# A spectral layer whose inverse-transform factors are made on 16 lines instead of being copied from 8 lines to 8 others

## Chip, cores and metric

The kernel runs on one core of a Trainium2 chip. The metric is the device time of one launch in microseconds (us): the median of several runs. The launch does the whole computation, and nothing is computed outside it.

## What is computed

The input x is 8 images of 8 channels of 512 x 512 in fp32. Two layers are applied, each to a group-normalised copy (4 groups of 2 channels) and added to its input. Layer 0 is the one that this change touches:

```
xs  = gn(x)[:, :, ::2, ::2]                        # 256 x 256
FW1 = rfft2(xs)                                    # only 8 row modes (0..3, -4..-1) x 4 column modes are used
out2[b,o,y,x] = sum_i FW1[b,i,y,x] * w[i,o,y,x]    # complex: a mix of the 8 channels, per mode
tmp = einsum('boxw,xz->bozw', out2, exp(lam1 * X)) # back to 512 rows
x2  = einsum('bozw,wi->bozi', tmp, exp(lam2 * T))  # back to 512 columns
x   = x + real(x2) / (256 * 256)
```

Layer 1 is a coupled map lattice (15 steps, each a 3x3 convolution per channel), a hidden 3x3 convolution to 128 channels with a 1x1 convolution back to 8, and a gate that mixes both; its result is added to the layer's input. Nearly all of the work is in layer 1.

## The kernel before, in words

**Stages of one image.** Each of the 8 images is an `Element`. Its layer 0 is a generator, `layer0`, that yields after each small piece of work. Its layer 1 is the lattice in two halves of four channels (`Half`; per half 15 steps over five sets k = 0..4 of 4 x 32 rows), 128 hidden rounds (`Hidden.round`, and `Hidden.point` after every two) and 43 gates (`Gate`).

**Ticks.** The time of an image is cut into 75 ticks. Tick t convolves the sets n = 2t and n = 2t + 1: n below 75 belongs to the first half, from 75 on to the second, with step n % 75 // 5 + 1 and set n % 5. The function `work` writes one tick: two convolutions (L533, TensorE), their settling (L588 on VectorE, L594 on ScalarE), transfers (`feed`, then `fetch`), up to two hidden rounds (L633, then L639 on ScalarE and L641 on VectorE), `squares`, then `others.first`, `Hidden.point` (L652) and `others.second`. The last two give left-over PSUM banks to the gates of the image before or to pieces of layer 0 of the image after. Pieces of layer 0 of the image after start at tick 24 (in the first image at once, as there are no gates to do). The order of each engine's instructions is the order of the source: `keep_order` ties every instruction to the one before it on its engine. There are four pairs of PSUM banks, named `pair`.

**The change of halves.** Ticks 35 to 37 run step 15 of the first half, and the second of tick 37's sets is already step 1 of the second half. In these ticks `leave` stores the finished sets (L574, `cml<-m`, four transfers for each set, issued one tick after the set), and `fetch` loads the drives of the second half (L491, `dE<-xn` and `dO<-xn`, eight transfers for each set). For each set of the second half, `square` takes a buffer for m from the pool `sets` (15 buffers, first in first out), clears the edge columns on GpSimd (L512) and squares the even drive into it on ScalarE (L513). Such a buffer is often one that a store L574 is still reading, so L512 waits for that store.

**One queue for transfers.** All transfers after the constants are issued by SyncE (SP), in the order of the source.

**The modes in layer 0.** For each channel L336 multiplies the image rows, as the stationary operand, with `dft_y`: 16 columns, 8 cosine and 8 negated sine columns, one per row mode. L340 copies the result to `mys`. After the statistics, L350 takes the mean out of row mode 0 and L353 scales. L361 makes the column modes: its stationary operand is 8 columns of `mys`, so the result lies on 8 lines (partitions), one per row mode. L366 copies it to `f`; `total` (L371, L375, L377) mixes channels on 8 lines, first the real part (`re`), then the imaginary (`im`). The inverse transform over rows (`over_rows`, L398) has a contraction of 16: lines 0 to 7 of `e1` are cosines, lines 8 to 15 sines. So its stationary operand `om` needs re and im on lines 0 to 7 (L387, L388) and -im and re on lines 8 to 15. L389 and L390 make the latter on lines 0 to 7 in `of_sin`, and a transfer on SP carries them to lines 8 to 15:

```
nc.sync.dma_start(out=om[8:, :, :8], in_=of_sin)   # L391
yield LATER
```

Then `over_rows(c)` runs L398 for channel c (the first channel in the tick's left-over slot right after; `LATER` only asks for the first bank of a slot), L402 on ScalarE copies the PSUM bank to `ty`, and `synthesis` (L430, L433, L435) adds the result to x. `om` holds 32 columns per channel, 8 of them used, the rest zero.

Of the kernel before, what the change touches and what calls it, by code (L numbers as in the profile page):

```python
# [35 lines left out]
F32 = mybir.dt.float32  # L36
AF = mybir.ActivationFunctionType
ALU = mybir.AluOpType
# [3 lines left out]
P = 128  # L42
C = 8
N = 512
NS = N // 2
# [40 lines left out]
def shape_constants():  # L86

    ky = np.array([0, 1, 2, 3, -4, -3, -2, -1])
    kx = np.arange(4)
    c = {}  # L90
    p, j = np.arange(P)[:, None, None], np.arange(2)[None, :, None]
    a = 2 * np.pi * ((ky * (2 * p + j)) % NS) / NS
    c["dft_y"] = np.concatenate([np.cos(a), -np.sin(a)], axis=2)
    a = 2 * np.pi * ((kx * (P * j + p)) % NS) / NS
    re = np.concatenate([np.cos(a), -np.sin(a)], axis=2)
    im = np.concatenate([np.sin(a), np.cos(a)], axis=2)
    c["dft_x"] = np.stack([re, im], axis=2)
    waves = np.zeros((8, 4))
    waves[:, 0] = ky / NS
    waves[:, 1] = np.concatenate([kx, -kx]) / NS  # L100
    waves[:4, 2] = 0.25
    c["waves"] = waves
    i, o = np.arange(P)[:, None] % SLAB, np.arange(SLAB)[None, :]
    c["shift"] = np.stack([i - o == d - 1 for d in range(3)], axis=1)
    p = np.arange(P)
    c["ends"] = np.stack([p % SLAB == 0, p % SLAB == SLAB - 1, p == 0, p == P - 1], axis=1)
    c["group_of"] = (np.arange(P)[:, None] % C) // 2 == np.arange(G)[None, :]
    return {k: np.ascontiguousarray(v, dtype=np.float32) for k, v in c.items()}
# [12 lines left out]
def view(t, offset, dims):  # L121

    return bass.AP(tensor=t.tensor, offset=t.offset + offset, ap=[list(d) for d in dims])
# [3 lines left out]
def conv_layers(ctx: ExitStack, tc: tile.TileContext, a, out):  # L127
    nc = tc.nc
# [3 lines left out]
    cp = ctx.enter_context(tc.tile_pool(name="const", bufs=1))  # L132
    dram = ctx.enter_context(tc.tile_pool(name="dram", bufs=1, space=bass.MemoryType.DRAM))
    sm = ctx.enter_context(tc.tile_pool(name="small", bufs=1))
# [22 lines left out]
    def row(shape, name):  # L157
        return wk.tile(shape, F32, tag="row", name=name, bufs=2)
# [19 lines left out]
    def load(name, shape):  # L178
        t = cp.tile(shape, F32, name=name)
        nc.scalar.dma_start(out=t, in_=a[name])  # L180
        return t
# [7 lines left out]
    xs_first = [load_x(sets, 0, c) for c in range(C)]  # L189


    dft_y = load("dft_y", [P, 2, 16])
    dft_x = load("dft_x", [P, 2, 2, 8])
    waves = load("waves", [8, 4])
    group_of = load("group_of", [P, G])
    ends = load("ends", [P, 4])
    w_p = load("w_p", [P, 3, 2, HID])
# [18 lines left out]

    e1 = cp.tile([16, N], F32, name="e1")
    e2 = cp.tile([P, N], F32, name="e2")
    om = cp.tile([16, C, 32], F32, name="om")
    nc.gpsimd.memset(om, 0.0)  # L220
    grid = {}
    for name in "XT":
# [3 lines left out]
    def sines():  # L226
        u, k, t = (sets.take([8, N], name) for name in ("u", "k", "sines"))
        rd = sm.tile([8, 1], F32, name="rd")
        for to, name, col, shift in (
            (e1[:8], "X", 0, 0.25), (t, "X", 0, 0.0), (e2[:8], "T", 1, waves[:, 2:3])  # L230
        ):
            xr = grid[name]
            nc.vector.tensor_tensor(rd, xr[:, 2:3], xr[:, 0:1], ALU.subtract)
            nc.vector.reciprocal(rd, rd)
            nc.vector.tensor_tensor(rd, rd, waves[:, col : col + 1], ALU.mult)
            nc.vector.tensor_scalar(u, xr, rd, shift, ALU.mult, ALU.add)
            nc.vector.tensor_scalar(k, u, MAGIC, None, ALU.add)
            nc.vector.tensor_scalar(k, k, MAGIC, None, ALU.subtract)
            nc.vector.tensor_tensor(u, u, k, ALU.subtract)
            nc.scalar.activation(to, u, AF.Sin, scale=6.283185)  # L240
        nc.scalar.dma_start(out=e1[8:], in_=t)
        for j in range(1, 4):
            nc.scalar.dma_start(out=e2[32 * j : 32 * j + 8], in_=e2[:8])
        for tile_ in (u, k, t, *grid.values()):
            sets.drop(tile_)
# [72 lines left out]
    def layer0(e, bank):  # L318


        def one():
            return bank[-1][:, 0]

        st = sm.tile([P, C, 4, 6], F32, name="st")
        mys = sm.tile([P, C, 2, 16], F32, name="mys")


        for c in range(C):
            yield c
            xt = e.x[c]  # L330
            for j in range(4):
                nc.vector.bn_stats(st[:, c, j], xt[:, j])
            my = one()[:, :32].rearrange("p (h k) -> p h k", h=2)
            for h in range(2):
                for j in range(2):
                    nc.tensor.matmul(  # L336
                        my[:, h], xt[:, 2 * j, h * NS : (h + 1) * NS : 2], dft_y[:, j],
                        start=(j == 0), stop=(j == 1),
                    )
            nc.scalar.copy(mys[:, c], my)  # L340
            e.done_with(c)
# [4 lines left out]
        lift = sm.tile([P, G], F32, name="lift")  # L346
        nc.vector.tensor_scalar(lift, mean, float(NS), None, ALU.mult)
        for g in range(G):
            at = mys[:, 2 * g : 2 * g + 2]
            nc.vector.tensor_scalar(  # L350
                at[:, :, :, 0], at[:, :, :, 0], lift[:, g : g + 1], None, ALU.subtract
            )
            nc.vector.tensor_scalar(at, at, rstd[:, g : g + 1], None, ALU.mult)  # L353
        wmix, ts = row([8, 2, C, C, 4], "wmix"), row([8, 2, C, C, 4], "ts")
        nc.sync.dma_start(out=wmix, in_=a["wmix"])
        yield LATER
        mx = one()[:, : C * 8].rearrange("p (c k) -> p c k", k=8)
        for c in range(C):
            for h in range(2):
                for q in range(2):  # L360
                    nc.tensor.matmul(  # L361
                        mx[:8, c], mys[:, c, h, q * 8 : (q + 1) * 8], dft_x[:, h, q],
                        start=(h + q == 0), stop=(h + q == 2),
                    )
        f = sm.tile([8, C, 2, 4], F32, name="f")
        nc.vector.tensor_copy(f, mx[:8].rearrange("p c (q k) -> p c q k", q=2))  # L366


        def total(q0, v0, q1, v1, op, name):
            for i, (q, v) in enumerate(((q0, v0), (q1, v1))):  # L370
                nc.vector.tensor_tensor(  # L371
                    ts[:, i], f[:, :, q].unsqueeze(2).to_broadcast([8, C, C, 4]), wmix[:, v],
                    ALU.mult,
                )
            nc.vector.tensor_tensor(ts[:, 0], ts[:, 0], ts[:, 1], op)  # L375
            t = sm.tile([8, C, 4], F32, name=name)
            nc.vector.tensor_reduce(t, ts[:, 0].rearrange("k i o m -> k o m i"), AX.X, ALU.add)  # L377
            return t

        yield LATER  # L380
        re = total(0, 0, 1, 1, ALU.subtract, "re")
        yield LATER
        im = total(0, 1, 1, 0, ALU.add, "im")

        of_sin = sm.tile([8, C, 8], F32, name="of_sin")
        s = 1.0 / (NS * NS)
        nc.vector.tensor_scalar(om[:8, :, 0:4], re, s, None, ALU.mult)  # L387
        nc.vector.tensor_scalar(om[:8, :, 4:8], im, s, None, ALU.mult)  # L388
        nc.vector.tensor_scalar(of_sin[:, :, 0:4], im, -s, None, ALU.mult)  # L389
        nc.vector.tensor_scalar(of_sin[:, :, 4:8], re, s, None, ALU.mult)  # L390
        nc.sync.dma_start(out=om[8:, :, :8], in_=of_sin)  # L391
        yield LATER


        def over_rows(c):
            ps = one()
            for at in range(0, P, 32):
                nc.tensor.matmul(  # L398
                    ps[at : at + 32], om[:, c], e1, start=True, stop=True, tile_position=(0, at)
                )  # L400
            ty = row([P, P, 4], "ty")
            nc.scalar.copy(ty.rearrange("k p j -> k (p j)"), ps)  # L402
            return ty
# [21 lines left out]
        def synthesis(ty, xt, st, half):  # L425
# [8 lines left out]
            for i in range(2):  # L434
                nc.vector.bn_stats(st[:, 2 * half + i], xt[:, 2 * half + i])  # L435

        ty_next = over_rows(0)
        closing = None
        for c in range(C):
# [416 lines left out]
    for i in range(3):  # L856
        xn = dram.tile([NP + 1, C, N], F32, name=f"xn{i}")
        cml, nca = (dram.tile([NP, C, N], F32, name=f"{name}{i}") for name in ("cml", "nca"))
        for plane in (xn, cml, nca):
            nc.scalar.dma_start(  # L860
                out=view(plane, 0, [[(NP - 1) * C * N, 2], [N, C], [1, N]]), in_=zrow
# [10 lines left out]
    for n in count():  # L872
        if n == C:
            sines()
            bands()
        if not e.pieces:
            break
        e.spectral(next(turns), 0, 0)
        tick()

        while e.stored >= C // 2 and len(e.first.loads) > 8 * (SETS - 2) and sets.free:
            e.first.load(nc.sync)
# [132 lines left out]
```

## Time and profile before

| what | value |
|---|---|
| median of 3 runs | 9992.99 us (9989.27 to 10003.49) |
| the profiled execution, its own time | 9988.58 us |
| its span | 9986.8 us |
| TensorE (PE) busy | 9359.6 us, 94% |
| VectorE (DVE) busy | 5869.1 us, 59% |
| ScalarE (ACT) busy | 4297.8 us, 43% |
| GpSimd (POOL) busy | 1755.5 us, 18% |
| mean granted TensorE clock | 0.983 |
| transfers by SyncE, share of the 16 DMA engines | 52.0% |

A line of the waits view says which engine and line waited, for whom, for how long in total, how often, and the longest of them. A line of the timeline gives start, duration, engine, line, operation, output<-inputs and count; in brackets stands the idle time of the engine just before it, and who ended it. `SPq` is SyncE issuing transfers; a DMA issue's duration is the issue alone.

### The profile page before, as it was taken

Reading aid. Unit: us, or ns where it says so; the run is one execution under the profiler, and the core shown is the slowest. Engines: PE = TensorE matmul, PEld = TensorE weight load, DVE = VectorE, ACT = ScalarE, POOL = GpSimd, SP = SyncE. Lnnn points to the kernel's source line nnn. Section 1 sums busy time; section 2 is a strip of 40 time slices with the busy share of each in tenths; the row PEclk is TensorE's granted clock in tenths of the full one; section 3 lists DMA queues with packets and bytes.
Section 4 is the critical chain, followed back from the end, with each engine's and each line's share of the span. In section 5 each row is a group of like instructions: output and inputs, shape, how many; then the busy total and the mean of one; then the engine's idle time right before and its main releaser. Section 6 shows DMA issues by size and latency. Waiting matters only on the chain. (4 is left out here: it accounts for less than half of the span.)

```text
span 9986.8 us, 353049 instructions
## 1 busy us (share of the span) xinstructions
PE 9359.6 (94%) x160496; PEld 4296.7 (43%) x160496; DVE 5869.1 (59%) x6067; ACT 4297.8 (43%) x4445; POOL 1755.5 (18%) x1406
## 2 busy tenths in 40 slices
PE   6999999899998999989999899999999899998999
PEld 2444444443444444444444444444434444444433
DVE  5665555665566655666556655566555565555555
ACT  2444444444444434444344443444434354344422
POOL 2010111103121031101312013120121202211212
PEclk9999999999999999999999999999999999999999
DMA  4241355447544565445665356552566526753688
GB/s 147 88 120 34 82 140 134 134 127 168 139 128 136 126 163 137 133 124 135 159 144 141 112 141 162 141 158 94 143 160 145 155 91 144 168 129 94 150 199 200
DMA packets 625562, 1353.48 MB, mean 136 GB/s; under 512 B 73066, under 2 KB 73194, under 8 KB 594050
## 3 DMA queue, kind: packets, MB, share of 16 engines
q1 hardware_dynamic: 621728, 1329.77, 52.0%
q8 instruction: 1261, 20.66, 0.9%
q14 instruction: 235, 1.93, 0.1%
q10 hardware_dynamic: 2338, 1.13, 0.0%
HBM read 992.27 MB, written 268.78 MB: 126 GB/s over the span
## 5 line engine op out<-in xcount | busy, mean ns | idle before, releaser
L533 PE MATMUL pair<-m,band 32*32 32x512 f32 x115200 | 4096.7, 605 | 200.2 <-issue 96.0
L594 ACT ACTIVATE m<-m 128x1024 f32<-128x1024 f32 x2240 | 2363.7, 1055 | 2795.7 <-DVE m L588 2674.2
L533 PEld LDWEIGHTS pair<-m,band 32*32 32x32 f32 x115200 | 2262.4, 103 | 1941.3 <-issue 970.0
L633 PE MATMUL pair<-cols,w_p 32*128 32x511 f32 (+1 forms) x24576 | 2866.2, 603 | 41.4 <-DMA cols<-xn 14.2
L588 DVE SCALAR_TENSOR_TENSOR m<-pair,dO 128x1024 f32<-128x1024 f32 x1280 | 1507.2, 1219 | 1478.0 <-PE pair L533 1294.2
L633 PEld LDWEIGHTS pair<-cols,w_p 32*128 32x128 f32 x24576 | 1270.8, 186 | 1651.0 <-issue 1123.3
L588 DVE SCALAR_TENSOR_TENSOR m<-pair,dE 128x1024 f32<-128x1024 f32 x1120 | 1319.1, 1219 | 1068.6 <-PE pair L533 878.3
L641 DVE TENSOR_SCALAR h<-pair,b_p 128x1024 f32<-128x1024 f32 x1024 | 1312.9, 1283 | 810.8 <-PE pair L633 803.3
L639 ACT ACTIVATE h<-pair,b_p 128x1024 f32<-128x1024 f32 x1024 | 1140.3, 1114 | 1043.4 <-PE pair L633 1043.0
L652 PE MATMUL pair<-h,w_u 128*32 128x512 f32 x8192 | 996.5, 598 | 136.4 <-DVE h L641 123.5
L726 POOL TENSOR_TENSOR mix<-mix 96x512 f32<-96x512 f32 x344 | 437.4, 1271 | 3757.9 <-ACT mix L724 3551.2
L703 PE MATMUL pair<-gin,w_g 128*32 128x511 f32 (+1 forms) x8256 | 964.1, 600 | 33.3 <-DMA gin<-nca 17.0
L708 POOL TENSOR_TENSOR mix<-mix 96x512 f32<-96x512 f32 x344 | 443.4, 1289 | 2050.6 <-DMA mix<-nca 1340.1
L598 POOL TENSOR_SCALAR dO<-dO 128x2048 f32<-128x2048 f32 x80 | 431.9, 5410 | 1225.6 <-DVE m L588 1225.5
L652 PEld LDWEIGHTS pair<-h,w_u 128*32 128x32 f32 x8192 | 249.4, 110 | 757.1 <-issue 384.0
L703 PEld LDWEIGHTS pair<-gin,w_g 128*32 128x32 f32 x8256 | 235.3, 110 | 711.2 <-issue 472.2
L665 ACT ACTIVATE y<-y,b_u 128x512 f32<-128x512 f32 x256 | 184.7, 721 | 808.0 <-DVE y L661 807.8
L731 DVE SCALAR_TENSOR_TENSOR mix<-mix,back 96x512 f32<-96x512 f32 x344 | 335.7, 976 | 148.5 <-POOL mix L726 148.5
L659 ACT COPY y<-pair 128x512 f32<-128x512 f32 x256 | 149.7, 585 | 605.1 <-PE pair L652 482.8
L713 DVE TENSOR_SCALAR mix<-pair,b_g 128x512 f32<-128x512 f32 x344 | 258.0, 750 | 251.6 <-PE pair L703 251.4
L720 PE MATMUL pair<-mix,w_g 128*32 128x512 f32 x2064 | 356.8, 593 | 9.6 <-DVE mix L713 7.8
L526 POOL TENSOR_SCALAR dO<-dO,base 128x512 f32<-128x512 f32 x320 | 237.0, 756 | 453.8 <-DMA dO<-xn 323.0
(86 smaller groups left out, 2643.8 us busy)
## 6 DMA issues: line engine op xcount, KB each, us to landing
gin<-xn SPq DMA_DIRECT2D x344, 384.0 KB
cols<-xn SPq DMA_DIRECT2D x256, 512.0 KB
x<-in_x SPq DMA_DIRECT2D x120, 1024.0 KB
gin<-cml SPq DMA_DIRECT2D x344, 320.0 KB
gin<-nca SPq DMA_DIRECT2D x344, 320.0 KB
dE<-xn SPq DMA_DIRECT2D x320, 256.0 KB
dO<-xn SPq DMA_DIRECT2D x320, 256.0 KB
mix<-xn SPq DMA_DIRECT2D x344, 192.0 KB
```

The lines of the kernel that those rows point to most:

```text
L533: nc.tensor.matmul(ps[h // 2][32 * t : 32 * t + 32, h % 2], band[at, c0 + (t if step % 2 else h), dx], m[at, t, dx : dx + N], start=(n == ...
L588: nc.vector.scalar_tensor_tensor(u[:, at], ps[q], FLOOR, d[:, at], ALU.max, ALU.add)
L594: nc.scalar.square(u[:, at], u[:, at])
L598: nc.gpsimd.tensor_scalar(d, d, 0.5, None, ALU.add)
L633: nc.tensor.matmul(ps[g // 2][:, g % 2, lo:hi], w_p[p, dx, i % 2], self.cols[p, i // 2, at : at + hi - lo], start=(n == 0), stop=(n == 2), ...
L639: nc.scalar.activation(h[:, :2], ps[0], AF.Relu, bias=b_p)
L641: nc.vector.tensor_scalar(h[:, 2:], ps[1], b_p, 0.0, ALU.add, ALU.max)
L652: nc.tensor.matmul(ps[32 * g : 32 * g + 32], w_u[:, r % 4], h[:, g], start=(r == self.hs[0][0]), stop=(r == self.hs[-1][0]), tile_position ...
L703: nc.tensor.matmul(ps[32 * j : 32 * j + 32, lo:hi], gband[:, dx], gin[:, j, at : at + hi - lo], start=(n == 0), stop=(n == 2), tile_positi ...
L708: nc.gpsimd.tensor_tensor(d, d, ng, ALU.subtract)
L720: nc.tensor.matmul(ps[at], gpoint[:, at], mix[:, 3], start=True, stop=True, tile_position=(0, 32 * j),)
L726: nc.gpsimd.tensor_tensor(d, d, mix[: GR * C, 2], ALU.mult)
```

## The change

The row modes are made twice: `dft_y` has each of its cosine and sine columns two times, so `mys` has 32 columns per half instead of 16, and L361's stationary operand has 16 columns, which puts the same modes on lines 0 to 7 and again on lines 8 to 15. `wmix`, `ts`, `f`, `re`, `im` get 16 lines. Two columns of constants, `on_cos` (1/NS^2 on lines 0 to 7, 0 elsewhere) and `on_sin` (-1/NS^2 on lines 8 to 15, 0 elsewhere), select what each line needs, so four VectorE instructions write all 16 lines of `om`. `of_sin` and the transfer of L391 are gone. `om` is packed to 8 columns per channel; L398 still reads 32 columns, of which 24 now belong to the next three channels (or to three channels of zeros at the end), and the lines of the result that they make are not read.

```diff
-    c["dft_y"] = np.concatenate([np.cos(a), -np.sin(a)], axis=2)
+    c["dft_y"] = np.concatenate([np.cos(a), np.cos(a), -np.sin(a), -np.sin(a)], axis=2)
...
+    waves[:8, 3] = 1.0 / (NS * NS)
+    waves[8:, 4] = -1.0 / (NS * NS)
...
-    om = cp.tile([16, C, 32], F32, name="om")
+    om = cp.tile([16, C + 3, 8], F32, name="om")
...
-        mys = sm.tile([P, C, 2, 16], F32, name="mys")
+        mys = sm.tile([P, C, 2, 32], F32, name="mys")
...
-            my = one()[:, :32].rearrange("p (h k) -> p h k", h=2)
+            my = one()[:, :64].rearrange("p (h k) -> p h k", h=2)
...
-                at[:, :, :, 0], at[:, :, :, 0], lift[:, g : g + 1], None, ALU.subtract
+                at[:, :, :, 0:9:8], at[:, :, :, 0:9:8], lift[:, g : g + 1], None, ALU.subtract
...
-        wmix, ts = row([8, 2, C, C, 4], "wmix"), row([8, 2, C, C, 4], "ts")
+        wmix, ts = row([16, 2, C, C, 4], "wmix"), row([16, 2, C, C, 4], "ts")
...
-                        mx[:8, c], mys[:, c, h, q * 8 : (q + 1) * 8], dft_x[:, h, q],
+                        mx[:16, c], mys[:, c, h, q * 16 : (q + 1) * 16], dft_x[:, h, q],
...
-        of_sin = sm.tile([8, C, 8], F32, name="of_sin")
-        s = 1.0 / (NS * NS)
-        nc.vector.tensor_scalar(om[:8, :, 0:4], re, s, None, ALU.mult)
-        nc.vector.tensor_scalar(om[:8, :, 4:8], im, s, None, ALU.mult)
-        nc.vector.tensor_scalar(of_sin[:, :, 0:4], im, -s, None, ALU.mult)
-        nc.vector.tensor_scalar(of_sin[:, :, 4:8], re, s, None, ALU.mult)
-        nc.sync.dma_start(out=om[8:, :, :8], in_=of_sin)
+        on_cos, on_sin = waves[:, 3:4], waves[:, 4:5]
+        back = sm.tile([16, C, 4], F32, name="back_re")
+        nc.vector.tensor_scalar(back, re, on_sin, -1.0, ALU.mult, ALU.mult)
+        nc.vector.tensor_scalar(re, re, on_cos, None, ALU.mult)
+        nc.vector.scalar_tensor_tensor(om[:, :C, 0:4], im, on_sin, re, ALU.mult, ALU.add)
+        nc.vector.scalar_tensor_tensor(om[:, :C, 4:8], im, on_cos, back, ALU.mult, ALU.add)
         yield LATER
...
-                    ps[at : at + 32], om[:, c], e1, start=True, stop=True, tile_position=(0, at)
+                    ps[at : at + 32], om[:, c : c + 4].rearrange("p c k -> p (c k)"), e1, start=True, stop=True, tile_position=(0, at)
```

The array `wmix` in memory holds its 8 lines twice. In the program's order the change leaves the number of instructions of TensorE, VectorE, ScalarE and GpSimd as it was and takes 8 issues, one per image, out of SP's queue.

More of the change, by code (lines that the diff above doesn't have):

```diff
@@ L97, in shape_constants @@
     c["dft_x"] = np.stack([re, im], axis=2)
-    waves = np.zeros((8, 4))
-    waves[:, 0] = ky / NS
-    waves[:, 1] = np.concatenate([kx, -kx]) / NS
+    waves = np.zeros((16, 5))
+    waves[:8, 0] = ky / NS
+    waves[:8, 1] = np.concatenate([kx, -kx]) / NS
     waves[:4, 2] = 0.25
+    waves[:8, 3] = 1.0 / (NS * NS)
+    waves[8:, 4] = -1.0 / (NS * NS)
     c["waves"] = waves
@@ L189, in conv_layers @@
     xs_first = [load_x(sets, 0, c) for c in range(C)]
-    dft_y = load("dft_y", [P, 2, 16])
+    dft_y = load("dft_y", [P, 2, 32])
     dft_x = load("dft_x", [P, 2, 2, 8])
-    waves = load("waves", [8, 4])
+    waves = load("waves", [16, 5])
     group_of = load("group_of", [P, G])
@@ L229, in sines @@
         for to, name, col, shift in (
-            (e1[:8], "X", 0, 0.25), (t, "X", 0, 0.0), (e2[:8], "T", 1, waves[:, 2:3])
+            (e1[:8], "X", 0, 0.25), (t, "X", 0, 0.0), (e2[:8], "T", 1, waves[:8, 2:3])
         ):
@@ L234, in sines @@
             nc.vector.reciprocal(rd, rd)
-            nc.vector.tensor_tensor(rd, rd, waves[:, col : col + 1], ALU.mult)
+            nc.vector.tensor_tensor(rd, rd, waves[:8, col : col + 1], ALU.mult)
             nc.vector.tensor_scalar(u, xr, rd, shift, ALU.mult, ALU.add)
@@ L361, in layer0 @@
                     nc.tensor.matmul(
-                        mx[:8, c], mys[:, c, h, q * 8 : (q + 1) * 8], dft_x[:, h, q],
+                        mx[:16, c], mys[:, c, h, q * 16 : (q + 1) * 16], dft_x[:, h, q],
                         start=(h + q == 0), stop=(h + q == 2),
                     )
-        f = sm.tile([8, C, 2, 4], F32, name="f")
-        nc.vector.tensor_copy(f, mx[:8].rearrange("p c (q k) -> p c q k", q=2))
+        f = sm.tile([16, C, 2, 4], F32, name="f")
+        nc.vector.tensor_copy(f, mx[:16].rearrange("p c (q k) -> p c q k", q=2))
         def total(q0, v0, q1, v1, op, name):
@@ L371, in total @@
                 nc.vector.tensor_tensor(
-                    ts[:, i], f[:, :, q].unsqueeze(2).to_broadcast([8, C, C, 4]), wmix[:, v],
+                    ts[:, i], f[:, :, q].unsqueeze(2).to_broadcast([16, C, C, 4]), wmix[:, v],
                     ALU.mult,
@@ L375, in total @@
             nc.vector.tensor_tensor(ts[:, 0], ts[:, 0], ts[:, 1], op)
-            t = sm.tile([8, C, 4], F32, name=name)
+            t = sm.tile([16, C, 4], F32, name=name)
             nc.vector.tensor_reduce(t, ts[:, 0].rearrange("k i o m -> k o m i"), AX.X, ALU.add)
@@ L992 @@
         "T": i["T"],
-        "wmix": w12.transpose(2, 4, 0, 1, 3),
+        "wmix": np.tile(w12.transpose(2, 4, 0, 1, 3), (2, 1, 1, 1, 1)),
         "K": i["K_local"].reshape(C, 9),
```

## Prediction

> **What bounds the kernel now.** First the page: TensorE (PE) is busy 94% of the span. Then the waits view for PE alone, as only what PE waits for can shorten the span, and its view by the tile `om`, which shows the operations around the removed transfer.
>
> ```profile
> PE 9359.6 (94%) x160496; PEld 4296.7 (43%) x160496; DVE 5869.1 (59%) x6067; ACT 4297.8 (43%) x4445; POOL 1755.5 (18%) x1406
> ```
>
> ```profile
> PE pair L652 <- DVE h L641: 123.5, 140, 1.6
> PE pair L398 <- DMA om<-of_sin: 117.1, 8, 24.4
> PE pair L533 <- issue: 96.0, 58, 5.2
> PE pair L533 <- ACT m L513: 64.8, 20, 10.6
> ```
>
> PE is idle 9986.8 - 9359.6 = 627 us in all, and 117.1 us of it is eight waits for the one transfer that the change removes. Asked window by window, they are 6.7 us (start, at 64 us), 3.0 (at 360 us), and then 15.1, 24.4, 18.8, 17.6, 15.1 and 16.4 us (images 1 to 6, sum 107.4). Why the last six are so long shows in the timeline of the first of them:
>
> ```profile
> 1840.92 0.16 DVE L387 TENSOR_SCALAR om<-re 8x32 f32<-8x32 f32 x1
> ...
> 1841.48 3.94 SPq L491 DMA_DIRECT2D dE<-xn  x4
> 1846.38 3.45 SPq L491 DMA_DIRECT2D dO<-xn  x4
> 1850.89 0.77 SPq L391 DMA_DIRECT2D om<-of_sin  x1
> 1851.95 7.63 SPq L574 DMA_DIRECT2D cml<-m  x8
> ...
> 1856.48 1.20 PE L398 MATMUL pair<-e,om 16*32 16x512 f32 x4 [15.13 <-DMA om<-of_sin]
> ```
>
> VectorE had the factors by 1841.8; the transfer of 2 KB stood in SP's queue behind eight drive loads, went out at 1850.9 and landed at 1856.4. The view by windows gives the DMA engines a share of 0.98 to 1.00 from 1800 to 1860 there: it is a burst of loads and stores at the change of halves. So the next question is what else PE needs from this burst. The same timeline, a tick later:
>
> ```profile
> 1860.38 0.11 POOL L512 MEMSET m<- 128x8 f32 x1 [17.09 <-DMA cml<-m]
> 1863.08 0.11 POOL L512 MEMSET m<- 128x8 f32 x1 [2.59 <-DMA cml<-m]
> ```
>
> ```profile
> 1872.10 3.88 ACT L513 ACTIVATE m<-dE,mhalf 128x2048 f32<-128x2048 f32 x2
> 1875.88 0.57 ACT L402 COPY ty<-pair 128x512 f32<-128x512 f32 x1
> ...
> 1876.51 4.10 PE L533 MATMUL pair<-m,band 32*32 32x512 f32 x116 [0.79 <-ACT ty L402]
> ```
>
> Tick 38's convolutions need two squares (L513), these need L512, and L512 waits for the stores L574. Today the second L512 is done at 1863.2 and its square is wanted at about 1874: the wait for `om` hides this one. The last image has no layer 0 after it, so no `om`, and shows what lies beneath:
>
> ```profile
> 9071.29 0.11 POOL L512 MEMSET m<- 128x8 f32 x1 [14.42 <-DMA cml<-m]
> 9071.43 2.00 ACT L513 ACTIVATE m<-dE,mhalf 128x2048 f32<-128x2048 f32 x1 [8.91 <-POOL m L512]
> ...
> 9073.49 9.25 PE L533 MATMUL pair<-m,band 32*32 32x512 f32 x192 [10.57 <-ACT m L513]
> ```
>
> [...] where the queue is free: from issue to PE's start took 2.2 us (61.98 to 64.22) and 2.0 us (357.91 to 359.91); in the burst it took 5.6. [...] after the wait of 15.1 us 183 records of L533 took 8.20 us, after the wait of 3.0 us 6.70 us. [...]
>
> **The change part by part.**
>
> *Removed:* eight L391 and their waits. *Taking their place at PE:* L398 waits for VectorE's four small instructions. L387 to L390 took 0.16 us each, about 0.1 us apart when nothing disturbs them; the two forms with a second tensor I price at L283's row (128x8, 0.222 us). So `om` is ready within 1 us of where `of_sin` was. PE's last work before the wait ended at 1841.3, the four would end at about 1841.8: 0.5 us at most instances, 1.5 in image 3, where L390 took 1.44 us. Queued behind L398 is all of PE, but in images 1 to 6 this half microsecond falls into the wait below.
>
> *Images 1 to 6, the new last wait.* PE resumes about 15 to 24 us earlier and does tick 37 without a new need of the burst: its sets were squared before, its columns (`cols`) loaded since 1820. In tick 38 its fifth record waits for L402 (`ty`), which stands on ScalarE behind both squares. From the second L512 on: 0.14 us to the square (9071.29 to 9071.43), 2.0 us for it, 0.57 us for the copy with 0.1 overlap, 0.05 to PE: 2.65 us. So tick 38 starts at (second L512) + 2.65 us at the earliest. Its start before, less that floor, is the gain if L512 doesn't move:
>
> | image | L533 after `ty` | second L512 | gain |
> |---|---|---|---|
> | 1 | 1876.51 | 1863.08 | 10.8 |
> | 2 | 3098.09 | 3082.49 | 13.0 |
> | 3 | 4323.89 | 4308.70 | 12.5 |
> | 4 | 5549.31 | 5535.07 | 11.6 |
> | 5 | 6767.36 | 6752.11 | 12.6 |
> | 6 | 7993.02 | 7977.85 | 12.5 |
>
> The sum is 73.0 us, each below its `om` wait, so the floor binds in all six. L574 stands right behind L391: with that gone it can be issued up to 1.06 us earlier (1850.89 against 1851.95)[...]. I take 0.7: + 4.2 us (1.2 to 6.4).
>
> *Slow restart.* PE now idles for some us at tick 38 and runs its first records at the low clock: 9.25 us for 192 records in the last image against 6.74 warm (at 7905), 2.5 us; the 15 us wait above cost 1.5[...]. I take 1.5 for each: - 9.0 us (0 to -16).
>
> *What is late next.* The squares of sets 3 and 4 (L513 at 1889.45) wait for the store of the first half's last set, which is issued after that tick's `cols` load. It comes earlier too, but meets the end of the burst: I put its landing at about 1872 to 1874 (it was 1879.5), and the squares shift to about 1877. Some 4 us remain, so 0; the other end is in the second rival.
>
> *Start and image 0.* At the start the chain is bare: 61.9 to 64.2, less four L353 that are longer by 64 elements [...]: + 2.0. In image 0: PE free at 356.9, `om` ready at about 358, before 359.9: + 1.8. Together 3.8.
>
> *Added PE work.* L336 has 512 records in all (16 columns more each). Eight took 1.11 us, 0.14 each; the load of 128 columns fills most of that. [...] 0 to 3.4 us, I take 1.7. L361: 64 pairs took 1.65 us (26 ns each), with 8 columns more to load[...]; 0 (up to 2). L340 gets 32 elements more, about 0.03 us on ScalarE (43% busy), nothing on the path; without that cover 64 x 0.03 = 2 us. [...] `om`'s packing leaves L398 at 32 columns: 0.
>
> *Sum:* 73.0 + 4.2 - 9.0 + 3.8 - 1.7 = 70 us (56 to 84 with the ends as I think they combine). The profiled execution's 9988.58 would become 9918; the median of the runs, 4.4 us above it, 9923.
>
> **The rivals.**
>
> *A, all of the wait goes.* If the stores land much earlier without L391, or buffers turn out to be others, PE gets 107.4 - 3 for `om`, + 3.8, + up to 9 for a clock that stays up: 108 to 117, so 9880. Against it speak the six L512 times and the last image. 6%.
>
> *B, more is given back.* The last image has a second wait of 5.45 us at 9088 for the squares of sets 3 and 4. If images 1 to 6 get it too, 6 x 5.45 = 33 us are lost: 9956, and up to 9971 with a second slow restart of 2.5 us each. Against it: here two hidden rounds (5.4 us) stand between the two convolutions, there they don't. 11%.
>
> *C, slower: the doubled row modes.* PE is the bound, and L336 grows. It eats the gain at 70/512 = 0.137 us more per record, and is slower by 0.2% from 0.176. An L336 record takes 0.268 us from end to end now and is issued every 0.14 us. Only if 16 columns more doubled that would this decide, say 10015. 3%.
>
> That the transfer isn't really removed is excluded by the program's order: SP has 8 issues less.
>
> **How the numbers follow.** My case has 80%, with 9909 to 9937 as its own range. The range of 8 in 10 takes in B's lower end and a little of the way to A: 9898 to 9957. 0.2% (20 us) is about what a measurement can tell here. My case, A and nearly all of B are faster by more: 0.93; 0.04 within; 0.03 slower.
>
> **What would show it.** Right: PE's waits no longer name `om<-of_sin`, L398 <- VectorE is below 10 us in all, and about 4 to 12 us of idle appear in each of images 1 to 6 before L533, released by ACT m L513 or ACT ty L402, with L512 still ended by `cml<-m`, the second of them within about 1 us of where it stood relative to the drive loads. L336's eight records stay at about 1.1 us. Wrong: no wait at L513 or `ty` (A), a second wait for L513 some 15 us later (B), L336 near 2 us (C), or L398 waiting several us for VectorE.

## The result and the profile after

The changed kernel took 9905.70 us (median of 4 runs, 9902.76 to 9917.57) beside 9998.24 us for the kernel before (4 runs, 9989.27 to 10005.24): ratio 0.9913, 95% interval 0.9902 to 0.9925. The profiled execution took 9903.73 us with a span of 9901.9 us, 84.9 us less than the span before. The prediction said 9923 us with a range of 9898 to 9957: the median lies inside it, and 3 us below the narrower range (9909 to 9937) that it gave its own case. In the changed kernel the lines after the constants stand two or three lower: L533 is L536, L512 is L515, L513 is L516, L398 is L401, L402 is L405, L652 is L655, L336 is L338, L361 is L363.

The page's first line, then the waits view for PE (us in total, number of waits, longest):

```profile
PE 9355.4 (94%) x160496; PEld 4299.0 (43%) x160496; DVE 5876.2 (59%) x6067; ACT 4301.9 (43%) x4445; POOL 1762.5 (18%) x1406
```

```profile
PE pair L655 <- DVE h L644: 124.7, 141, 1.9
PE pair L536 <- issue: 99.6, 59, 4.9
PE pair L536 <- ACT m L516: 69.7, 21, 11.8
PE pair L401 <- DVE om L393: 20.0, 8, 5.3
PE pair L536 <- ACT ty L405: 8.1, 6, 2.8
```

PE's work is what it was (9355 against 9360 us); its idle time fell from 627 to 546 us. The wait of 117.1 us for the transfer became one of 20.0 us for VectorE. Smaller increases stand beside it: the waits for L516 and `ty` together grew by 8.3 us (from 64.8 and 4.7), those put down to "issue" at L536 by 3.6 (by 13.0 over all lines of PE, from 110.7 to 123.7).

The timeline of image 1 shows the new wait for `om`:

```profile
1833.41 2.22 POOL L529 TENSOR_SCALAR dE<-dE,base_e 128x512 f32<-128x512 f32 x2 [2.27 <-ACT m L516]
1833.52 0.61 DVE L391 TENSOR_SCALAR re<-re,waves 16x32 f32<-16x32 f32 x1
...
1834.17 1.49 DVE L392 SCALAR_TENSOR_TENSOR om<-im,waves,re 16x32 f32<-16x32 f32 x1
1835.59 0.23 DVE L393 SCALAR_TENSOR_TENSOR om<-im,waves,back_re 16x32 f32<-16x32 f32 x1
1835.88 0.63 PE L401 MATMUL pair<-e,om 16*32 16x512 f32 x4 [2.20 <-DVE om L393]
```

and a tick later the floor that the prediction computed, the two clearings and what follows the second:

```profile
1853.07 0.11 POOL L515 MEMSET m<- 128x8 f32 x1 [17.44 <-DMA cml<-m]
...
1855.60 0.11 POOL L515 MEMSET m<- 128x8 f32 x1 [2.42 <-DMA cml<-m]
...
1855.74 2.00 ACT L516 ACTIVATE m<-dE,mhalf 128x2048 f32<-128x2048 f32 x1 [0.52 <-POOL m L515]
1857.65 0.56 ACT L405 COPY ty<-pair 128x512 f32<-128x512 f32 x1
...
1858.26 8.05 PE L536 MATMUL pair<-m,band 32*32 32x512 f32 x188 [1.08 <-ACT ty L405]
```

From the second clearing to PE: 1858.26 - 1855.60 = 2.66 us; predicted 2.65.

**A yardstick for all that follows.** In each of images 1 to 6, take the interval from the end of PE's last record before `om` (L655, until 1833.7 in image 1) to its first convolution record after `ty` (1858.3 there). The sum of the six is "inside", the rest of the span "outside". The start and image 0 count as outside.

| profiled execution | inside, us | PE idle inside | outside, us |
|---|---|---|---|
| before | 229.2 | 112.1 | 9757.6 |
| changed | 152.1 | 33.9 | 9749.8 |
| changed, two more executions | 146.9, 152.0 | 33.3, 39.6 | 9748.4, 9753.3 |

So 77.1 of the 84.9 us came from inside, 7.8 from outside. Of the 7.8, 5.2 us are time in which PE was busy (9242.4 and 9237.2 us outside), the rest idle time.

### The profile page after: what moved, and what is told of

The parts are those of the page before. It is cut to its first block, busy times and chain, and to the rows that moved or that the text cites. A ratio compares the mean times of both kernels' runs of the same rounds, so it can differ in the third digit from the quotient of the medians.

```text
span 9901.9 us, 353033 instructions
## 1 busy us (share of the span) xinstructions
PE 9355.4 (94%) x160496; PEld 4299.0 (43%) x160496; DVE 5876.2 (59%) x6067; ACT 4301.9 (43%) x4445; POOL 1762.5 (18%) x1406
## 3 DMA queue, kind: packets, MB, share of 16 engines
q8 instruction: 1261, 20.66, 0.9%
## 5 line engine op out<-in xcount | busy, mean ns | idle before, releaser
L536 PE MATMUL pair<-m,band 32*32 32x512 f32 x115200 | 4093.8, 605 | 212.5 <-issue 99.6
L536 PEld LDWEIGHTS pair<-m,band 32*32 32x32 f32 x115200 | 2258.3, 103 | 1955.8 <-issue 983.1
L636 PE MATMUL pair<-cols,w_p 32*128 32x511 f32 (+1 forms) x24576 | 2862.1, 603 | 47.0 <-issue 15.9
L655 PE MATMUL pair<-h,w_u 128*32 128x512 f32 x8192 | 995.0, 598 | 136.2 <-DVE h L644 124.7
L655 PEld LDWEIGHTS pair<-h,w_u 128*32 128x32 f32 x8192 | 249.0, 110 | 756.7 <-issue 384.7
L529 POOL TENSOR_SCALAR dO<-dO,base 128x512 f32<-128x512 f32 x320 | 238.6, 763 | 437.1 <-DMA dO<-xn 246.3
```

The source lines that it names most:

```text
L536: nc.tensor.matmul(ps[h // 2][32 * t : 32 * t + 32, h % 2], band[at, c0 + (t if step % 2 else h), dx], m[at, t, dx : dx + N], start=(n == ...
L636: nc.tensor.matmul(ps[g // 2][:, g % 2, lo:hi], w_p[p, dx, i % 2], self.cols[p, i // 2, at : at + hi - lo], start=(n == 0), stop=(n == 2), ...
L655: nc.tensor.matmul(ps[32 * g : 32 * g + 32], w_u[:, r % 4], h[:, g], start=(r == self.hs[0][0]), stop=(r == self.hs[-1][0]), tile_position ...
```

## The experiments

The theory was the prediction's: the transfer is late because it stands behind the drive loads on SP's queue and meets full DMA engines (a share of 0.98 to 1.00 there), and what the change gains is cut by the clearing of m. The rivals: the transfer itself is what costs; the doubled modes cost; something else takes the time back. All ratios are to the kernel before on the same chip. The runs of the kernel before had medians of 9989.91, 10004.15 and 9991.21 us in the three groups in which the experiments ran.

**1. The transfer kept, from another queue** (before, L391 issued by ScalarE):

```diff
-        nc.sync.dma_start(out=om[8:, :, :8], in_=of_sin)
+        nc.scalar.dma_start(out=om[8:, :, :8], in_=of_sin)
```

> The kernel before with one word changed: the transfer of the sines' factors is issued by ScalarE instead of SP. Theory (the transfer was late because of its place in SP's queue): it goes out at once and lands 2 to 6 us after of_sin, so PE waits 2 to 6 us for it in images 1 to 6 instead of 15 to 24, the squares and the ty copy behind them then set the same floor as in the changed kernel, and the time falls by 70 to 95 us. Rival (the 16 DMA engines are full, so any transfer is late there): the waits stay above 10 us each and the gain is below 45 us.

Measured: 9942.12 us (4 runs), ratio 0.9954 (0.9938 to 0.997), a gain of 48 us: between the two. PE still waited 52.0 us for the transfer, in 7 waits. Its timeline, image 1 (`ACTq` is ScalarE issuing):

```profile
1840.93 0.73 ACTq L391 DMA_DIRECT2D om<-of_sin  x1
...
1846.44 1.20 PE L398 MATMUL pair<-e,om 16*32 16x512 f32 x4 [6.01 <-DMA om<-of_sin]
...
1847.46 9.39 PE L533 MATMUL pair<-m,band 32*32 32x512 f32 x183
```

The transfer was issued as soon as VectorE had written `of_sin` (0.03 us later in every image). In images 1 to 6 it then took 5.5 to 7.9 us from its issue to PE, with the DMA engines' share at 0.60 to 0.91 meanwhile; at the start and in image 0 of the kernel before it had taken 2.2 and 2.0 us, with a share of 0.02. In the kernel before, the transfer stood 61.7 us in SP's queue, summed over the six images (7.8 to 15.9 us each), and that is what the other queue took away: the six waits fell from 107.4 to 45.6 us. What is left is the flight past the other transfers, longer than the theory had it. PE came back slowly: 183 records in 8.1 to 9.4 us, waits for instructions left out, where 6.95 us is their time at the full granted clock. But so it did in the kernel before (8.1 to 8.7) and in five of the six images of the changed kernel (8.1 to 9.2; 6.95 in image 1), so this is not what sets the three apart. Inside fell to 175.5 us, 53.7 less than before; outside hardly moved (9759.5).

**2. The doubled modes alone** (changed kernel, but `om` from `re` and `im` on lines 0 to 7, and lines 8 to 15 by a transfer on SP again):

```diff
...
+        of_sin = sm.tile([8, C, 8], F32, name="of_sin")
+        s = 1.0 / (NS * NS)
+        nc.vector.tensor_scalar(om[:8, :C, 0:4], re[:8], s, None, ALU.mult)
...
+        nc.sync.dma_start(out=om[8:, :C], in_=of_sin)
```

> The changed kernel with its doubled row modes and 16 lines, but with om made on 8 lines and carried to lines 8 to 15 by the transfer on SP, as before. It measures the cost of the doubled modes alone. Theory: 0 to 5 us slower than the kernel before, PE's waits for om again 15 to 24 us in images 1 to 6. Rival (the wider modes cost TensorE or the copies something that the removed wait hides): 15 us slower or more.

Measured: 9988.29 us (12 runs) against 9989.91 (17 runs), ratio 0.9995 (0.9987 to 1.0004). The wait was back:

```profile
PE pair L402 <- DMA om<-of_sin: 103.2, 7, 20.4
```

So what the change adds costs nothing that can be told (13 us gained to 4 lost), though each L338 record took 282 ns where L336's took 268, and L363's weight loads 93 where L361's took 87. Rival C falls. The gain of the change comes from PE's not having to wait for the transfer.

**3. The changed kernel with the burst spread** (a call of `fetch` issues at most 8 drive loads; it had been up to 16):

```diff
-            while n >= -11 and self.loads and (self.loads[0][2] or sets.free):
-                self.load(nc.sync)
+            for _ in range(8):
+                if n >= -11 and self.loads and (self.loads[0][2] or sets.free):
+                    self.load(nc.sync)
```

> The changed kernel, with fetch issuing at most eight drive loads in a tick, so that the stores of the finished sets stand behind 8 loads in SP's queue instead of 16. Theory (what is left is the floor of the second clearing of m, which waits for those stores): the second clearing comes 6 to 9 us earlier relative to PE, PE's waits for the squares or ty in images 1 to 6 (10 us in all in the changed kernel's trace) go to below 3 us, the last image's wait of 19.8 us falls below 12, and the time falls by 8 to 25 us against the changed kernel. Rival (the burst is bound by its bytes, or the loads now come too late in the next tick): same as the changed kernel within 5 us, or slower with waits for dE or dO.

Measured: 9875.96 us (4 runs), ratio 0.9881 (0.9862 to 0.99), beside the changed kernel as it is:

> The changed kernel again, for a second trace and a tighter comparison on the same chip as the others. Expected 0.9913 of the kernel before within 0.0015; the first record of L401 waits about 2.2 us for VectorE in each of images 1 to 6 again if that wait has a cause in the program and isn't chance.

which took 9897.08 us (5 runs), ratio 0.9911 (0.9894 to 0.9927). The timeline of image 1 of the spread version (its second clearing, then tick 38; L516 here is the clearing):

```profile
1844.29 0.54 POOL L516 MEMSET m<- 128x8 f32 x1 [2.41 <-PE pair L537]
...
1854.42 0.56 ACT L405 COPY ty<-pair 128x512 f32<-128x512 f32 x1
1855.03 6.54 PE L537 MATMUL pair<-m,band 32*32 32x512 f32 x188 [0.79 <-ACT ty L405]
```

The second clearing began 10.7 us before tick 38, not 2.66; counted from the interval's start it came 8.3 to 11.9 us earlier than in the changed kernel (6 to 9 were expected). PE idled 0.8 us there (4.7 us in the six images, where below 3 was expected), the last image's waits for squares fell from 19.8 to 8.8 us, and no image restarted slowly (6.54 us for 188 records in four of them, the other two broken by a wait put down to "issue"). Inside fell from 152.1 to 131.6 us: the floor had cost the changed kernel 20 us, and a late store, not layer 0, set it. The gain of 21 us on the changed kernel is within what was expected.

**4. The same limit in the kernel before**, transfer and all:

> The kernel before with one edit: a call of the fetch issues at most 8 drive loads, so L391's transfer stands behind 8 loads on SP's queue and not 16, and its engines carry half the burst. Theory (the wait was the transfer's place in the queue plus full DMA engines, and the late clearing of m was the burst too): TensorE's wait for om falls from 117 us to 40-70 us and the time to 9925-9955 us, faster than the kernel with the transfer on ScalarE's queue or like it, but 50-80 us slower than the changed kernel with the same limit. Rival (the transfer itself[...] was the wait, or the burst doesn't matter to it): om wait stays above 90 us and the time within 20 us of the kernel before.

Measured: 9899.42 us (4 runs), ratio 0.9892 (0.9873 to 0.9911), as fast as the changed kernel without the limit (0.9911 to 0.9923). The waits for `om` behaved as the theory had it, the time did not: 25 us below its range.

```profile
PE pair L398 <- DMA om<-of_sin: 55.9, 8, 11.2
PE pair L534 <- ACT m L514: 55.3, 18, 5.5
```

Nor did the transfer stand behind 8 loads, as had been expected: in three of the six images it was issued 0.03 us after VectorE's work, and its time in the queue was 8.1 us in all, not 61.7. The changed kernel with the same limit was only 38 us faster (9861.60 us, see 5), not 50 to 80.

Run again beside the changed kernel, and with L391 on ScalarE as well:

> The kernel before with the limit of 8 loads, again, beside the changed kernel on the same chip, as its 105 us were far above what was expected. Theory (half the burst takes 61 us of the om wait, about 15 us of L534's wait for m, and the cold clock with them): ratio 0.988-0.990 again, level with the changed kernel or up to 15 us below it. Rival (its first run was favoured by chance): 0.992-0.994, where the expectation of its first run had it.

> The kernel before with both small edits: at most 8 drive loads in a call of the fetch, and L391 issued by ScalarE. Theory (of the transfer only its place in SP's queue and the full DMA engines cost time; with both eased the change has little left to bring): TensorE's wait for om falls to 25-40 us (2 to 6 us in each image) and the ratio to the kernel before to 0.985-0.988, level within 10 us with the changed kernel with the limit (0.986 and 0.9881). Rival (the transfer costs a full flight of 5.5 us and a cold clock in each image whatever its queue): om wait 45-55 us, ratio 0.989-0.991, level with the limit alone.

> The changed kernel as it is, on the same chip as the two others: ratio 0.990-0.992 as in its two first runs; om wait 20.0 us in 8 waits. If fetch stalls of TensorE are a property of the program and of its DMA load, L536's waits put down to issue are 96-106 us again, and all of 1 us or more of them lie on the same place of a 256-instruction grid.

Measured in one group: 9898.77 us, ratio 0.9909 (0.9892 to 0.9925), for the limit alone; 9897.74, ratio 0.9906 (0.9888 to 0.9924), with the other queue too; 9910.38, ratio 0.9923 (0.9907 to 0.9938), for the changed kernel. The second run of the limit alone fell just outside what the theory gave it (as did the changed kernel, 0.9923 against 0.990 to 0.992; its wait for `om` was 20.0 us again, and L536's "issue" waits 103.4); the gain of the limit is 92 to 105 us. The two edits together brought no more than one: the wait for `om` stayed where it was,

```profile
PE pair L398 <- DMA om<-of_sin: 54.5, 7, 10.7
```

so on the wait and the ratio the rival was right: with half the burst the queue place no longer matters (8.1 and 5.6 us in the two runs of the limit alone), and the flight through busy DMA engines does: 5.5 to 10.3 us in the six images here (in the first run of the limit alone their share was 0.89 to 0.98 over the six bursts). PE came back slowly in every image, too, 183 records in 8.3 to 9.3 us, as the rival had it. Inside was 173.5, 170.7 and 169.9 us in the three executions, 56 to 59 below the kernel before. Outside was 9715.4, 9708.7 and 9744.4; in the first two that is 42 and 49 us below the kernel before. Of it 18 and 19 us are PE's waits for ScalarE, and 12 us in each are shorter PE work on the same records (their mean granted clock was 0.987, that of the kernel before 0.983). No single wait holds the rest, and part of it is chance (see 5).

**5. VectorE's slow operation taken out** (changed kernel; the second set of y factors is turned by i, so that lines 8 to 15 get -im and re from the row transform; two scalings on 16 lines write `om`):

```diff
-    c["dft_y"] = np.concatenate([np.cos(a), np.cos(a), -np.sin(a), -np.sin(a)], axis=2)
+    c["dft_y"] = np.concatenate([np.cos(a), np.sin(a), -np.sin(a), np.cos(a)], axis=2)
...
-        nc.vector.scalar_tensor_tensor(om[:, :C, 0:4], im, on_sin, re, ALU.mult, ALU.add)
...
+        nc.vector.tensor_scalar(om[:, :C, 0:4], re, s, None, ALU.mult)
...
```

> The changed kernel with the second set of the y factors turned by i, so that lines 8 to 15 get (-im, re) straight from the row transform and om is written by two scalings on 16 lines; the two operations with two tensor inputs and the select constants are gone. Theory (VectorE's first such operation takes 1.49 us instead of 0.24 because GpSimd's drive addition runs beside it): TensorE's om wait falls from 20.0 us to 6-10 us, the om operations take 0.1-0.3 us each in every image. But three of six images are held at the floor that the second clearing of m sets, so that the time falls only by 3-7 us against the changed kernel, within what 5 rounds can barely tell. Rival (the 2.2 us is a cost of waking TensorE or of the form of om): om wait stays at 17-21 us, time as the changed kernel.

> The same with the fetch limited to 8 loads in a call. Here no image is held by the second clearing of m, so the shorter wait for om counts in full: 6 times 1.7 us, 9-11 us below the changed kernel with the limit alone, and 25-35 us below the changed kernel. Rival (another wait takes up the 1.7 us): within 3 us of the changed kernel with the limit alone.

> The changed kernel with the fetch limited to 8 loads in a call, again, on the same chip as the three others, so that 10 us can be told: 18-25 us below the changed kernel, ratio to the kernel before 0.986-0.990; om wait 20.0 us as in its first run, wait of L537 for m by L517 56 us. Rival (the first run's gain was chance): level with the changed kernel, 0.991.

Measured in one group: 9923.33 us, ratio 0.9919 (0.9904 to 0.9934); with the limit 9883.23, ratio 0.9879 (0.9864 to 0.9893); the changed kernel with the limit 9861.60, ratio 0.986 (0.9844 to 0.9877). The view by tile `om` shows the operation's times (min/median/max in ns), first of the changed kernel and then of this one:

```profile
L392 DVE SCALAR_TENSOR_TENSOR om<-im,waves,re x8: 240/1490/1492, 62.8 to 7880.0; 16x32 f32<-16x32 f32 x8
```

```profile
L389 DVE TENSOR_SCALAR om<-re x8: 158/159/290, 61.6 to 7891.9; 16x32 f32<-16x32 f32 x8
L390 DVE TENSOR_SCALAR om<-im x8: 169/170/179, 61.7 to 7892.0; 16x32 f32<-16x32 f32 x8
```

and the waits of this one (without the limit):

```profile
PE pair L533 <- issue: 125.1, 65, 4.2
...
PE pair L533 <- ACT m L513: 82.0, 27, 11.2
...
PE pair L398 <- DVE om L390: 5.4, 2, 4.5
```

The wait fell from 20.0 to 5.4 us, nearly all of it the start, so it was VectorE's work and no cost of waking PE. The times point to GpSimd's addition as what slowed VectorE; that the second tensor input makes an operation slow they do not show. In every one of images 1 to 6 of the changed kernel L391, with one tensor input, took 0.60 or 0.61 us and ended 0.03 us after the first of the two L529; L392, begun while the second ran, took 1.49 us and ended 0.03 us after that. In image 0, with GpSimd idle, they took 0.23 and 0.24. In image 3 of the changed kernel with the limit, the second run, the two changed places:

```profile
4232.63 1.49 DVE L391 TENSOR_SCALAR re<-re,waves 16x32 f32<-16x32 f32 x1
4234.15 0.24 DVE L392 SCALAR_TENSOR_TENSOR om<-im,waves,re 16x32 f32<-16x32 f32 x1
```

Here L391 was the one begun during GpSimd's long addition. The two scalings of the turned kernel began up to 0.15 us before GpSimd's addition, and were done in 0.16 and 0.17 us. So the turned kernel's gain came with VectorE work that was under way before GpSimd's; that this order decides, or that one tensor input would have helped, is not shown.

The theory on the time falls: without the limit nothing was gained (inside was 147.4 us, where the changed kernel had 146.9 to 152.1), and with it the run was 22 us slower in the same group, and level with the first run of the spread version by ratio (0.9881). Inside the gain is there: 131.7 became 118.3 us, 6 x 2.2. Outside it is lost: 9768.1 us against 9720.3 and 9751.9 in two executions of the same spread program. Of the 32 us between those two, 23 are PE's own work, which took 9338.9 us in the one and 9361.7 in the other for the same records, at a mean granted clock of 0.990 and 0.988. The clock record of a trace holds two values, 1.0 and 0.5 (51 stretches of each in the kernel before, 55 in the changed one): outside the six intervals PE was busy at 0.5 for 155 us in the one and 201 us in the other, and half of that difference is the 23 us. "Issue" is the one cause that is higher in both turned kernels than in all other profiles: 145 and 141 us over all lines of PE, where the eleven others have 99 to 126.

**What "issue" is.** An example from the changed kernel, timeline of PE alone:

```profile
3015.70 2.21 PE L536 MATMUL pair<-m,band 32*32 32x512 f32 x48
3019.16 4.51 PE L536 MATMUL pair<-m,band 32*32 32x512 f32 x128 [1.25 <-issue]
3027.57 1.09 PE L536 MATMUL pair<-m,band 32*32 32x512 f32 x16 [3.90 <-issue]
```

Between two such waits stand exactly 128 records, 256 instructions with their weight loads. The page's third part has a DMA queue of its own for instructions:

```profile
q8 instruction: 1261, 20.66, 0.9%
```

1261 packets of 16 KB; PE's instructions, counted in the trace, are 160496 weight loads, 160496 matmuls and 1936 semaphore operations, and 322928 / 256 = 1261.4. Numbered in order, PE's "issue" waits of more than 0.8 us fall on one and the same place of a grid of 256 instructions, give or take one: 43 of 43 in the kernel before, 51 of 52 in the changed one, 63 of 64 in the turned one. Matched with that queue's packets in the trace, PE went on 1.5 us (median; 1.25 to 1.75 in nine of ten) after a packet had landed, in all thirteen profiles (1.49 us in the kernel before, 1.47 in the changed one); by chance the last packet would have landed anywhere up to 7.9 us before, which is their mean distance. By these figures PE waits there for its own instructions. Most blocks cost no such wait: only 43 of some 1261 blocks in the kernel before and 51 in the changed one began with a wait of more than 0.8 us. Together the waits put down to "issue" were 99 to 145 us in a launch. What makes a block come late no run here shows, nor why the turned kernels have more of it.

## Why the prediction was right, and where not

*The new last wait* (73.0 + 4.2 us): right in its mechanism. Inside fell by 77.1 us against 77.2 predicted; that the two agree so closely is luck, as the images one by one show (and the two more executions of the changed kernel, 82.3 and 77.2):

| image | predicted (with 0.7 each) | measured | L536 after the second clearing |
|---|---|---|---|
| 1 | 11.5 | 10.6 | 2.66 |
| 2 | 13.7 | 20.2 | 2.67 |
| 3 | 13.2 | 13.4 | 3.10 |
| 4 | 12.3 | 12.4 | 3.27 |
| 5 | 13.3 | 9.8 | 3.37 |
| 6 | 13.2 | 10.8 | 2.67 |

The floor of 2.65 us is met in images 1, 2 and 6. In 3 to 5 PE came 0.4 to 0.7 us later than the floor, after waits for its own instructions of 2.0, 2.9 and 2.8 us in tick 37. The second clearing itself moved against the interval's start by between 2.1 us later and 7.2 us earlier (sum 6.0 earlier; predicted 0.7 earlier in each, 4.2 in all), so the sum was better than its parts. (The lower end of 1.2 us, 0.2 in each image, was the author's estimate: 2 KB at the 239 GB/s that the DMA engines moved from 1850.9 to 1856.5 take 0.01 us.) Experiment 3 is the proof of the floor: let the stores come earlier, and inside loses 20 us more. Two of the prediction's signs of being right did not come: L398's wait for VectorE was 20.0 us and not below 10, and PE's idle time just before L536 was 0.6 to 4.0 us in each image and not 4 to 12. PE spent the slack in the longer waits for VectorE and for its own instructions instead; the floor sets the end of the interval, whichever wait fills it.

*The wait for `om` on VectorE* (0.5 us, 1.5 in image 3): the size was wrong, 2.2 us in all six. The four operations were priced undisturbed (0.16 and 0.222 us; the two-tensor form took 0.24 at the start and in image 0). But L391 and L392 took 0.60 and 1.49 us and ended when GpSimd's two L529 did (1835.66 and 1835.63 us for L392). The lines before had shown it: L390, a scaling with one tensor input, took 0.59 us in five of the six images and 1.44 in image 3, each time ending 0.03 us after GpSimd's L526, and the prediction took image 3 for an exception.

```profile
1841.21 0.59 DVE L390 TENSOR_SCALAR of_sin<-re 8x32 f32<-8x32 f32 x1
...
4284.40 1.44 DVE L390 TENSOR_SCALAR of_sin<-re 8x32 f32<-8x32 f32 x1
```

What joins the two engines no run here shows, nor why it holds up one operation and not another: L389, begun 0.04 to 0.07 us after that same L526 in each of the six images, took 0.16 us. Not held up, a scaling of 16 lines took what one of 8 lines did, 0.16 us (median 159 ns for L389 of the turned kernel, 158 for L387 of the kernel before), as the prediction priced it. In images 1, 2 and 6 the 2.2 us fell into the floor's wait, as the prediction said of its half microsecond.

*Slow restart* (-9 us): mis-sized for this execution, not in kind. Only images 1 and 6 restarted at a lower clock (0.79 and 0.80 granted), 8.05 and 8.14 us for 188 records against 6.54: 3.1 us. Two more executions of the same program gave 3.1 and 9.9 us (two and five images), so the price of 9 us fits one execution and is three times what the two others lost. The price had no place for the short waits: after waits of 1.5 and 2.2 us with 1.9 us of work between them, five of the six images of the changed kernel ran the 183 records behind `om` at a granted clock of 0.80 to 0.90, in 8.1 to 9.2 us instead of 6.95. This lies inside the intervals, whose end is at or near the floor.

*What is late next* (0 us): right; no second wait for L516 in images 1 to 6, and rival B falls. What the step did not list is PE's waits put down to "issue": 9.7, 6.1 and 4.6 us inside in the three executions, where the kernel before had none. Why is not shown.

*Start and image 0* (+3.8): measured 0.8 us at the start (L401 at 63.4, L398 at 64.2) and 1.5 in image 0; L355 took 286 ns where L353 took 255. *Added PE work* (-1.7, the author's estimate, which no trace had shown): 0.9 us by the records (64 groups of eight grew from 1.116 to 1.130 us each; in the group at 7902 of the kernel before the weight loads were busy for 1.02 us), and within what experiment 2 allows. L363's records stayed at L361's 169 ns, and L342's copies took 204 ns where L340's took 177.

*The sum:* predicted 70, measured 84.9 between the spans and 92.5 between the medians. Inside is right to 0.1 us, by luck in its parts. The difference is outside: predicted -6.9, measured +7.8. Of these 14.7 us the restarts are 5.9. The other 9 are not assigned, and are small beside the 32 us by which two executions of one program, the spread version, differ outside; 23 of those are PE's own work at a lower mean clock (see 5).

*Rivals:* A would have needed the clearing out of the way, and that is experiment 3 (inside 131.6, time 9862 to 9876); in the changed kernel the floor held. C falls by experiment 2.

What the prediction did not see is how much of the trouble was the burst's and how little the transfer's. Halving the burst in the kernel before gives 92 to 105 us, about what the change gives (81 to 93 in three groups). With the burst halved, the change still takes inside from about 172 to 132 us; in the group that held both, the time went from 9899.42 to 9861.60. The fastest version of all is the changed kernel with the limit of 8 loads: 0.986 and 0.9881 of the kernel before.

## What to carry to other kernels

A long wait for a small transfer is first of all a question about what stands before it in its queue and what fills the DMA engines: limiting the loads per call gave as much here (92 to 105 us) as removing the transfer (81 to 93 us). Before counting a removed wait as gained, look for the next thing that the waiting engine needs from the same burst and compute its floor from that event's own time: here it held to 0.02 us in three images and 0.4 to 0.7 us in the others. And a small operation on VectorE is best priced from its own row in the trace before, in the images where GpSimd works beside it: L390 took 0.16 us with GpSimd idle (image 0) and 0.59 or 1.44 us beside L526.

## What the hardware showed that was not expected

- PE's "issue" waits point to its own instructions: nearly all of those above 0.8 us (43 of 43 before, 51 of 52 after) stand on one place of a 256-instruction grid and end about 1.5 us after a 16 KB packet lands; "issue" is 99 to 145 us of a span of 9.9 ms.
- A 2 KB transfer issued at once took 5.5 to 7.9 us to PE with the DMA engines' share at 0.60 to 0.91, and 2.0 to 2.2 us at a share of 0.02.
- In images 1 to 6 of the changed kernel L391 and L392, of 16x32 elements and begun while one of GpSimd's L529 ran, ended 0.03 us after it: 1.49 us for L392, with two tensor inputs (0.24 in image 0, with GpSimd idle), 0.60 us for L391, with one (0.23 in image 0; 1.49 in one image with the limit). L389 of the kernel before, begun 0.04 to 0.07 us into an L526, took 0.16 us.
- 16 columns more for each L336, and 8 more for each L361 weight load, cost 14 and 6 ns a record (268 to 282, 87 to 93), and no time of the launch that could be told (ratio 0.9995, experiment 2).
